# Moving VectorE's side steps next to the array steps in a two-layer mixture-of-experts and attention kernel

## The chip, the cores and the metric

The kernel runs on one core of a Trainium2 chip, in float32. The metric is the device time of one execution in microseconds (us), given as the median of several runs. The names used below: PE is TensorE, DVE is VectorE, ACT is ScalarE, POOL is GpSimd, and SP is the engine that issues most of the DMAs.

## The reference

The program is one "macaron" block on an input of 8 batches of 1024 tokens with 256 features each: half a feed-forward layer, attention, and half a feed-forward layer again, each on a layer-normed input and added to the residual.

```python
x = x + 0.5 * ffn(layernorm(x), ...)
x = x + attn(layernorm(x), ...)
x = x + 0.5 * ffn(layernorm(x), ...)

# attn: 16 heads of 16 features
xd = (x @ W_down).reshape(b, t, h, s)
keys, queries, values = per-head 16x16 products of xd      # keys and queries times 16 ** -0.25
attn = softmax(einsum('bqhs,bkhs->bhqk', queries, keys))
out = einsum('bhqk,bkhs->bqhs', attn, values) @ W_unify + b_unify

# ffn: each token goes to its best of 8 experts, which takes its first 320 tokens in order;
# the rest of the tokens go through a shared two-layer network
eid = argmax(softmax(xf @ router_w + router_b))
rank = place of the token among those of its expert
out = expert(xf) where rank < 320 else shared(xf)
```

## The kernel before, in words

**Three parts in a row.** The first feed-forward layer, the attention of all batches, and the second feed-forward layer. The change lies in the attention part, in `run` inside `attention`. It runs over 32 *pairs* `n`: pair `n` is batch `n // 4` and one of its 4 groups of four heads. Each pair has 16 *units* `u`, two halves of 8, and in each unit the program issues:

- for pair `n`, twelve matmuls `psc` (the scores of four heads for 128 keys and 512 queries, three matmuls each), followed on ACT by four exponentials `ex` of 128x512;
- for the next pair `n + 1`, eight matmuls `pm` of the same kind (the scores the other way round, so that the maximum over the keys can be taken along a row), followed on DVE by four reductions `halves`, one for each `pm` tile of 128x512;
- for the unit before, the four products `av` with the values (`weighed`), either in one piece of 512 columns, or in two of 256.

A unit is written out in two half units: `ORDERS[0]` (heads 0 and 1 of `psc`, 2 and 3 of `pm`), then `av`, then `ORDERS[1]` (the other heads), then the second piece of `av` or an array step. Tiles `psc` rotate through four PSUM banks, and tiles `pm` through three. The three banks of `pm` are shared with some array steps: the router's logits `pl`, the routing sums `places` and `behind`, and the output projection `pu` each take one.

At the start of each half of a pair (units 0 and 8) DVE also transposes and inverts the finished `av` (`turned`, `rec`, in `divide`), and for the second and fourth group of a batch transposes the scaled result once more (`ho`, one unit later). At the end of each half it forms the minima (`lowest`, three small instructions, then `lowturned`).

**Work beside the pairs.** Everything else in this part is a set of generators in a list `beside`: `prepare(b)` (projections of the next batch), `unify(b)` (output projection), `route(b)` (layer norm, router and slots of the second feed-forward layer for a finished batch), `stats(b)` (layer norm statistics of a later batch) and `biased(b)`. Each generator yields the kind of its next step: ARRAY (it begins with PE), DVE or POOL. `step(kind)` advances the most urgent generator that stands at this kind, and does nothing when there is none. `queue(n)` adds them: `unify` and `prepare` in a batch's first pair, `route` of the batch before in its second pair, to be done four pairs later. `done_by(n)` at the end of a pair runs whatever is overdue. After the last pair `done_by(PAIRS + G)` runs what is left of the last `route`, and then the second half of the last batch's `unify` is issued and the second feed-forward layer begins.

A `route(b)` is a fixed string of steps: eleven DVE steps of layer norm (`norm_steps`: eight with `bn_stats` and `bn_aggr`, three with four or six small instructions each for the inverse root), two POOL steps (four rows are normalized, L184), six ARRAY steps (transposes `ptrn`, `pl`, `pl` with `logits`, for each of two halves), two DVE steps (`top`, `hot`; then `best`, `chosen`), an ARRAY step (`places`, with `sums` on POOL and `place` on DVE), two DVE steps (`rank`, `past`, `counted`; then `row`), an ARRAY step (`behind`, with `sums` on POOL again), a DVE step (`slot`, `lost`), and eight POOL steps that send the rows out by indirect DMA.

**What sets the order.** PE, ACT and DVE run their instructions in the order in which the program issues them here (a manual schedule); only POOL and SP are ordered by the framework. A DVE step therefore stands behind the reductions of its unit and in front of those of the next.

**Which unit runs which step.** Before, `SLOTS_OF` holds two sets for each pair: units (modulo 8) for an ARRAY step and units for a DVE step. For the first two pairs of a batch these are 0, 1, 3, 5 and 2, 4, 6; for the last two pairs 0, 1, 4 and 2, 3, 5, 6. A unit without an ARRAY step runs a POOL step. In the last pair of all (`ahead` is false, there is no `pm` any more) each unit from 2 on runs an ARRAY step.

Of the kernel before, what the change touches and what calls it, by code (L numbers as in the profile page):

```python
# [21 lines left out]
TB = T // P  # L22
# [18 lines left out]
def macaron(  # L41
# [98 lines left out]
    ARRAY, DVE, POOL = 0, 1, 2  # L140
# [620 lines left out]
    def attention(use, weights, router):  # L761
# [11 lines left out]
        PAIRS, UNITS = B * G, 2 * TB  # L773


        SLOTS_OF = [((0, 1, 4), (2, 3, 5, 6)), ((0, 1, 3, 5), (2, 4, 6))]

        ORDERS = [
            [(kind, int(h)) for kind, h in order.split()] for order in (
# [139 lines left out]
        def fetch(n):  # L919

            b, g = divmod(n, G)
            rows = slice(g * 64, (g + 1) * 64)
            qt = qts[n] = use.pool.tile([P, T], F32R, tag=f"q{n % 3}", name=f"q_{n}")
            kt = kts[n] = use.pool.tile([P, 2, T], F32R, tag=f"k{n % 3}", name=f"k_{n}")
            for i in range(2):
                nc.sync.dma_start(
                    out=kt[:, i, :].bitcast(F32), in_=krows[b][i, rows].rearrange("r c t -> (r c) t")
                )
            nc.sync.dma_start(out=qt.bitcast(F32), in_=qrows[b][rows].rearrange("r c t -> (r c) t"))
# [79 lines left out]
        def weigh(n, u, exs, parts=(0, 1)):  # L1009

            b, g = divmod(n, G)
            q, c = divmod(u, TB)
            if (n, q) not in avs:
                avs[n, q] = use.av.tile([P, 512], F32, tag="av", name=f"av_{n}_{q}")
            cols = slice(256 * parts[0], 256 * (parts[-1] + 1))
            for h, ex in enumerate(exs):
                at = (c * HEADS + 4 * g + h) * V
                nc.tensor.matmul(  # L1018
                    avs[n, q][32 * h : 32 * h + 32, cols],
                    lhsT=vps[b % 2][:, at : at + 2 * S],  # L1020
                    rhs=ex[:, cols],
                    start=(c == 0),
                    stop=(c == TB - 1 and parts[-1] == 1),
                )
            if c == TB - 1:
                divide(n, q)
# [30 lines left out]
        def unify(b, start=0):  # L1057
            for t in range(start, TB, 2):
                ps = bank_v(f"pu_{b}_{t}")
                for i in range(2):  # L1060
                    q, at = divmod((t + i) * P, 512)
                    for g in range(G // 2):
                        nc.tensor.matmul(  # L1063
                            ps[:, i * D : (i + 1) * D],
                            lhsT=outs[b, g, q][:, at : at + P],
                            rhs=wu_sb[:, g, :],
                            start=(g == 0),
                            stop=(g == G // 2 - 1),
                        )
                two = xs[b][:, t : t + 2, :]  # L1070
                nc.vector.tensor_tensor(
                    two, two, ps.rearrange("p (t d) -> p t d", d=D), ALU.add
                )
                rows = slice(b * T + t * P, b * T + (t + 2) * P)
                nc.sync.dma_start(
                    out=ahead_of_last[rows].rearrange("(t p) d -> p t d", p=P), in_=two
                )
                yield
# [48 lines left out]
        def afterwards(n=0):  # L1127

            for _ in range(len(later) - n):
                later.pop(0)()  # L1130
# [5 lines left out]
        def due(kind):  # L1136
            return min((w for w in beside if w[1] == kind), key=lambda w: w[0], default=None)

        def step(kind):
            work = due(kind)  # L1140
            if work is None:
                return
            try:
                work[1] = next(work[2]) or ARRAY
            except StopIteration:
                beside.remove(work)

        def done_by(n):
            while any(by <= n for by, _, _ in beside):
                for kind in (POOL, DVE, ARRAY):  # L1150
                    if any(by <= n and what == kind for by, what, _ in beside):
                        step(kind)

        def queue(n):

            b, g = divmod(n, G)
            if n + 2 < PAIRS:
                fetch(n + 2)
            if 0 < n <= B - AHEAD + 1:

                again = AHEAD - 2 + n
                nc.vector.memset(xs[again][:, 0, :1], 0.0)
                reload(again)
                beside.append([G * (again - 1) - 1, DVE, stats(again)])
            if g == 0:
                if b > 0:
                    beside.append([n, ARRAY, unify(b - 1)])
                if b + 1 < B:
                    beside.append([n + 1, POOL, prepare(b + 1)])
            if g == 1 and b > 0:  # L1170
                beside.append([n + 4, DVE, route(b - 1)])

        def ones(i):
            vp = use.pool.tile([P, TB * HEADS * V + S], F32, tag=f"vp{i}", name=f"vp{i}")
            nc.gpsimd.memset(vp, 1.0)
            vps.append(vp)

        def zero_rows(i):
            m = use.pool.tile([P, 512], F32R, tag=f"m{i}", name=f"m{i}")
            nc.gpsimd.memset(m.bitcast(F32), 0.0)  # L1180
            ms.append(m)
# [48 lines left out]
        def run(own):  # L1230
            for i in range(2, 4):
                zero_rows(i)
            fetch(1)
            ones(1)
            last = None

            def weighed(parts=(0, 1)):
                if last is not None:
                    weigh(*last, parts=parts)

            for n in range(PAIRS):
                ahead = n + 1 < PAIRS
                if n == (B - 1) * G:
                    done_by(n)
                    use.pool = own
                    use.last.close()
                    router.open()

                queue(n)
                for u in range(UNITS):  # L1250
                    todo = {}
                    old = len(later)
                    slots = SLOTS_OF[n % G < 2]
                    if ahead:
                        passes(n, n + 1, u, ORDERS[0], todo)

                        other = u % TB in slots[0] and due(ARRAY) is not None

                        whole = other or u % TB < 2
                        weighed((0, 1) if whole else (0,))  # L1260
                        passes(n, n + 1, u, ORDERS[1], todo)
                        if other:
                            step(ARRAY)
                        elif not whole:
                            weighed((1,))
                    else:

                        passes(n, None, u, ORDER_OF_LAST, todo)
                        weighed()
                        other = False  # L1270
                        if u > 1:
                            step(ARRAY)
                        if u == TB + 3:
                            beside.append([n + 1, ARRAY, islice(unify(B - 1), 2)])
                    if u % TB in slots[1]:
                        step(DVE)
                    if not other:
                        step(POOL)
                    last = (n, u, [todo["ex", h] for h in range(4)])
                    afterwards(len(later) - old)  # L1280
                    if ahead and u % TB == TB - 1:
                        lowest(n + 1, u // TB)
                if ahead:
                    done_by(n)
            weighed()
            afterwards()
            done_by(PAIRS + G)
            for _ in unify(B - 1, TB // 2):
                pass
# [17 lines left out]
    use = Use()  # L1307
    weights, fill_weights = attention_weights(const)
    first_pair, run = attention(use, weights, layers[1])

    def beside_last(blocks, main):
# [102 lines left out]
```

## Time and profile before

| | |
|---|---|
| median of 3 runs | 2935.99 us (2933.0 to 2938.25) |
| the profiled execution | 2939.6 us, its span 2937.9 us |
| first `ex` of pair 0 | 662.2 us from the span's start |
| first `ex` of pair 31 | 2399.7 us |
| last `ex` | ends at about 2449.4 us |
| busy share of PE, DVE, ACT, POOL | 95%, 64%, 47%, 29% |
| mean granted TensorE clock | 0.981 |

The times of the profile are those of one execution, which was 3.6 us longer than the median. The attention part takes some 1790 us of the span. In it each pair takes between 49 and 61.5 us, and the length of a unit can be read from the starts of the `ex` instructions on ACT: two in a row after each half unit. A pair with `prepare` or `unify` steps takes 58 to 61 us, one with some steps of `route` 52 to 55 us, and one with DVE steps alone about 50 or 51 us. Busy shares of PE are those of matmuls whose ends are modelled, so a unit's length says more than they do.

### The profile page before, as it was taken

How to read it: one execution, taken by the hardware profiler on the slowest of the kernel's cores; microseconds unless marked ns; L12 is line 12 of the kernel's file. 1: busy time of each engine (PE TensorE's matmuls, PEld its weight loads, DVE VectorE, ACT ScalarE, POOL GpSimd, SP SyncE). 2: the span in 40 equal slices, each digit the busy share in tenths (PEclk: the TensorE clock that was granted, in tenths of full speed). 3: DMA queues.
4: the chain of work that ended last, by engine and by line, in shares of the span. 5: the costliest groups of instructions: out<-in, count | busy, mean ns of one | idle time of the engine just before them, and what ended most of it. 6: DMA issues, size and time to landing. Idle time of an engine off the chain costs nothing.

```text
span 2937.9 us, 56693 instructions
## 1 busy us (share of the span) xinstructions
PE 2799.3 (95%) x22066; PEld 1546.2 (53%) x22066; DVE 1883.1 (64%) x4189; ACT 1375.2 (47%) x2512; POOL 851.8 (29%) x1136
## 2 busy tenths in 40 slices
PE   4799999899999999999999999999999999999998
PEld 4567776454444444444444444444444445666775
DVE  7344223467897888888788788788788963212221
ACT  1111111207766666766766765766766663111111
POOL 3434433414001033123222321420420214432331
PEclk7799999999999999999999999999999999999999
DMA  7522553413112101301301301311321102321440
GB/s 224 152 83 78 176 187 99 161 47 121 53 58 97 67 24 60 124 24 56 128 24 52 133 24 42 125 41 39 125 80 38 39 3 73 128 61 49 150 147 28
DMA packets 163737, 251.47 MB, mean 86 GB/s; under 512 B 36737, under 2 KB 109698, under 8 KB 163458
## 3 DMA queue, kind: packets, MB, share of 16 engines
q1 hardware_dynamic: 144178, 196.93, 20.6%
q0 software_dynamic: 18432, 50.62, 5.1%
q8 instruction: 177, 2.90, 0.4%
q14 instruction: 102, 0.84, 0.1%
q10 hardware_dynamic: 848, 0.18, 0.0%
HBM read 144.10 MB, written 103.57 MB: 84 GB/s over the span
## 4 chain that ended last, share of the span: by engine, by line
PE 63%; DVE 13%; issue 1%; DMA 0%; POOL 0%; ACT 0%; POOLq 0%; DVEq 0%
PE psc L987 20%; PE av L1018 15%; DVE halves L1003 9%; PE pm L987 6%; PE pe_o L499 5%; PE ph_o L456 5%; PE pe_e L499 2%; PE ph_e L456 2%; PE pu L1063 2%; PE pxd L862 2%; PE pv L894 1%; DVE turned L1033 1%; PE pq L880 1%; PE pl L1091 1%; PE ptrn L832 0%
## 5 line engine op out<-in xcount | busy, mean ns | idle before, releaser
L1003 DVE TENSOR_REDUCE halves<-pm 128x1 f32<-128x512 f32 x2048 | 1309.3, 681 | 260.9 <-PE pm L987 239.6
L996 ACT ACTIVATE ex<-psc 128x512 f32<-128x512 f32 x2048 | 1111.4, 596 | 574.5 <-PE psc L987 570.9
L987 PE MATMUL pm<-k,q 32*128 32x512 f32 x4096 | 870.5, 448 | 50.6 <-DVE halves L1003 38.6
L987 PE MATMUL psc<-q,k 32*128 32x512 f32 x4096 | 791.8, 455 | 3.1 <-PEq L668 3.1
L1018 PE MATMUL av<-ex,vp 128*32 128x256 f32 (+1 forms) x6472 | 610.9, 449 | 0.0
L987 PEld LDWEIGHTS psc<-q,k 32*128 32x128 f32 x4096 | 326.6, 183 | 479.0 <-issue 423.1
L987 PEld LDWEIGHTS pm<-k,q 32*128 32x128 f32 x4096 | 374.9, 183 | 133.4 <-DVE halves L1003 107.3
L987 PE MATMUL psc<-m,ones_r 32*128 32x512 f32 x2048 | 406.9, 390 | 0.0
L456 PE MATMUL ph_o<-bT_o,oa 128*128 128x512 f32 x704 | 318.6, 601 | 7.1 <-DVE h_o L474 5.3
L499 PE MATMUL pe_o<-ob,h_o 128*128 128x256 f32 x1408 | 322.6, 386 | 0.0
L1041 POOL TENSOR_TENSOR ot<-turned,rec 128x256 f32<-128x256 f32 x64 | 39.7, 620 | 883.9 <-DVE rec L1036 875.6
L499 PEld LDWEIGHTS pe_o<-ob,h_o 128*128 128x128 f32 x1408 | 268.1, 193 | 48.5 <-issue 13.8
L1018 PEld LDWEIGHTS av<-ex,vp 128*32 128x32 f32 x6472 | 127.6, 108 | 298.3 <-issue 275.6
L456 PEld LDWEIGHTS ph_o<-bT_o,oa 128*128 128x128 f32 x704 | 131.2, 191 | 159.7 <-issue 147.4
L470 ACT ACTIVATE h_o<-ph_o,ob 128x512 f32<-128x512 f32 x88 | 60.5, 687 | 328.9 <-PE ph_o L456 305.0
L987 PEld LDWEIGHTS psc<-m,ones_r 32*128 32x128 f32 x2048 | 196.6, 184 | 13.0
L474 DVE TENSOR_SCALAR h_o<-ph_o,ob 128x512 f32<-128x512 f32 x88 | 65.9, 748 | 196.2 <-ACT h_o L470 179.4
L509 DVE SCALAR_TENSOR_TENSOR y_o<-pe_o,old_o 128x256 f32<-128x256 f32 x88 | 37.2, 423 | 205.8 <-PE pe_o L499 141.2
L499 PE MATMUL pe_e<-wb,h_e 128*128 128x256 f32 (+1 forms) x640 | 143.9, 381 | 0.0
L456 PE MATMUL ph_e<-bT_e,wa 128*128 128x320 f32 x512 | 140.6, 433 | 1.8 <-ACT bT_e L204 1.8
L204 ACT COPY bT_o<-pt_bT_o 128x1024 f32<-128x1024 f32 x22 | 22.3, 1012 | 250.8 <-PE pt_bT_o L200 225.9
L499 PEld LDWEIGHTS pe_e<-wb,h_e 128*128 128x128 f32 (+1 forms) x640 | 112.9, 179 | 16.4 <-issue 3.1
(183 smaller groups left out, 2385.1 us busy)
## 6 DMA issues: line engine op xcount, KB each, us to landing
k<-krows SPq DMA_DIRECT2D x64, 512.0 KB
wa<-in_w_dram SPq DMA_DIRECT2D x16, 1024.0 KB
wb<-in_w_dram SPq DMA_DIRECT2D x16, 1024.0 KB
krows<-kh SPq DMA_DIRECT2D x32, 512.0 KB
krows<-kl SPq DMA_DIRECT2D x32, 512.0 KB
q<-qrows SPq DMA_DIRECT2D x32, 512.0 KB
rows_o<-buf SPq DMA_DIRECT2D x88, 130.0 KB
x<-in_x_dram SPq DMA_DIRECT2D x8, 1024.0 KB
```

Source lines behind the costliest of these rows:

```text
L456: nc.tensor.matmul(ps[:, i * 512 : i * 512 + width], lhsT=wa[:, k, (m + i) * P : (m + i + 1) * P], rhs=xnt[:, k, c0:c1], start=(k == 0), s ...
L470: nc.scalar.activation(t[:, 0, : hi - lo], ps[:, lo - c0 : hi - c0], AF.Relu, bias=bias[:, m : m + 1],)
L474: nc.vector.tensor_scalar(t[:, 1, : hi - lo], ps[:, 512 + lo - c0 : 512 + hi - c0], bias[:, m + 1 : m + 2], 0.0, ALU.add, ALU.max,)
L499: nc.tensor.matmul(ps[lo - i * P : hi - i * P, :D], lhsT=of[:, lo - a : hi - a], rhs=w[:, m, :], start=(m == 0), stop=(m == MC - 1),)
L509: nc.vector.scalar_tensor_tensor(y[:n, :], ps[:n, :D], 0.5, olds[i][:n, :], ALU.mult, ALU.add)
L862: nc.tensor.matmul(ps, lhsT=wd_sb[:, k, m * P : (m + 1) * P], rhs=xnt[:, k, :], start=(k == 0), stop=(k == KC - 1),)
L987: nc.tensor.matmul(ps, lhsT=lhs, rhs=rhs, start=(len(left) + 1 == todo[kind, h, "of"]), stop=not left,)
L996: nc.scalar.activation(ex, ps, AF.Exp, scale=S ** -0.5)
L1003: nc.vector.tensor_reduce(halves[m][:, t, half, h : h + 1], ps, AX.X, ALU.max, negate=True)
L1018: nc.tensor.matmul(avs[n, q][32 * h : 32 * h + 32, cols], lhsT=vps[b % 2][:, at : at + 2 * S], rhs=ex[:, cols], start=(c == 0), stop=(c == ...
L1041: nc.gpsimd.tensor_tensor(outs_t[q][:, :, at : at + S].rearrange("p (t a) s -> p a t s", t=4), by[:, :, :S].rearrange("p (a t) s -> p a t ...
L1063: nc.tensor.matmul(ps[:, i * D : (i + 1) * D], lhsT=outs[b, g, q][:, at : at + P], rhs=wu_sb[:, g, :], start=(g == 0), stop=(g == G // 2 - 1),
```

## The change

The two sets become one: units for an ARRAY step. A unit that runs an ARRAY step then also runs two DVE steps, right after it. Any other unit runs a DVE step only at position 6 of a half (modulo 8), and in the last pair of all at each odd unit as well. In a batch's last two pairs the ARRAY units are 0 and 1 of each half, no longer 4. When no ARRAY step is due in a unit, `other` is false, and the unit runs no DVE step except at position 6.

```diff
-        SLOTS_OF = [((0, 1, 4), (2, 3, 5, 6)), ((0, 1, 3, 5), (2, 4, 6))]
+        SLOTS_OF = [(0, 1), (0, 1, 3, 5)]
...
-                        other = u % TB in slots[0] and due(ARRAY) is not None
+                        other = u % TB in slots and due(ARRAY) is not None
...
-                    if u % TB in slots[1]:
+
+                    if other:
+                        step(DVE)
+                        step(DVE)
+                    elif u % TB == TB - 2 or not ahead and u % 2:
                         step(DVE)
                     if not other:
                         step(POOL)
```

`TB` is 8, and `slots` is `SLOTS_OF[n % G < 2]` with `G` = 4. No instruction is added or taken away; the steps of the generators run in other units.

## The prediction

> **What bounds the kernel now.** The page first: busy shares, the chain that ended last, the costliest groups.
>
> ```profile
> PE 2799.3 (95%) x22066; PEld 1546.2 (53%) x22066; DVE 1883.1 (64%) x4189; ACT 1375.2 (47%) x2512; POOL 851.8 (29%) x1136
> ...
> PE 63%; DVE 13%; issue 1%; DMA 0%; POOL 0%; ACT 0%; POOLq 0%; DVEq 0%
> ...
> L1003 DVE TENSOR_REDUCE halves<-pm 128x1 f32<-128x512 f32 x2048 | 1309.3, 681 | 260.9 <-PE pm L987 239.6
> ...
> L987 PE MATMUL pm<-k,q 32*128 32x512 f32 x4096 | 870.5, 448 | 50.6 <-DVE halves L1003 38.6
> ```
>
> PE leads, and DVE is the only other engine on the chain, through `halves`. Next the timeline of ACT in pair 23, whose `ex` starts mark the half units:
>
> ```profile
> 1997.08 1.09 ACT L996 ACTIVATE ex<-psc 128x512 f32<-128x512 f32 x2 [0.35 <-PE psc L987]
> 1998.53 1.09 ACT L996 ACTIVATE ex<-psc 128x512 f32<-128x512 f32 x2 [0.37 <-PE psc L987]
> 2000.01 1.08 ACT L996 ACTIVATE ex<-psc 128x512 f32<-128x512 f32 x2 [0.40 <-PE psc L987]
> ...
> 2005.29 1.08 ACT L996 ACTIVATE ex<-psc 128x512 f32<-128x512 f32 x2 [0.84 <-PE psc L987]
> ...
> 2008.90 1.08 ACT L996 ACTIVATE ex<-psc 128x512 f32<-128x512 f32 x2 [0.35 <-PE psc L987]
> ```
>
> A quiet half unit is 1.47 us, a unit 2.94. Two reductions take 1.29, so DVE has 0.36 us per unit to spare, less than one `bn_stats` step (0.42 + 0.18). Unit 13, from 2005.29 to 2008.90, is 3.61 long. The timeline of DVE and PE says why:
>
> ```profile
> 2003.09 1.29 DVE L1003 TENSOR_REDUCE halves<-pm 128x1 f32<-128x512 f32 x2 [0.48 <-PE pm L987]
> 2004.30 0.20 DVE L236 COPY sums<-places 128x56 f32<-128x56 f32 x1
> 2005.73 0.22 DVE L308 TENSOR_TENSOR place<-sums,places 128x64 f32<-128x64 f32 x1 [1.23 <-POOL sums L238]
> 2005.87 2.58 DVE L1003 TENSOR_REDUCE halves<-pm 128x1 f32<-128x512 f32 x4
> 2006.61 0.18 PEld L987 LDWEIGHTS pm<-k,q 32*128 32x128 f32 x1 [0.36 <-DVE halves L1003]
> ```
>
> A `places` step holds DVE for 1.23 us while it waits for POOL. The next reductions stand behind it, the first ends at about 2006.5, and the second `pm` of the half unit after gets its bank only then. That is the mechanism to follow: DVE work between two sets of reductions costs PE nothing until it delays a reduction by more than about 0.3 us; beyond that it costs its length.
>
> **The change part by part.** I take each step's units from the order of the two programs. No instruction or DMA is added. For one batch (routing of batch b-1):
>
> (a) *Layer norm steps, pair 4b+1.* Before in units 2, 4, 6, 10, 12, 14 and on into the next pair; now two each in units 0, 1, 3, 5, 8 (beside `prepare`), one in 6. A `prepare` unit is 4.7 to 4.85 long, since the array step adds about 1.9 us of PE. Of this DVE has 1.5 idle: two steps of 0.60 fit. Unit 5 is only 3.94: I count 0.5 for it and the two after it. In unit 8, with `turned` and `rec` (0.71 + 0.25), the two long steps (six instructions of 0.17, 1.0 us each) spill 0.4. Before, these units cost nothing (2.80 to 3.08). Sum +0.9. No row shows two steps in such a unit: from 0 (all hidden) to 3 (five units by 0.6); I stay near 1 because the idle time can be read in the trace; less than nothing is excluded, as nothing is lost there now.
>
> (b) *Pair 4b+2 loses its DVE steps* (units 2, 3, 5, 6, 10) and gets four array steps in units 0, 1, 8, 9 instead of one in 12. By the `ex` starts, units of pair 22 with DVE work or its backlog took 3.22, 3.03, 3.59 and 3.57. New length, from units elsewhere with these steps: transposes 3.95 and 0.14 in the unit after, `pl` 3.80, `pl` in unit 8 4.21; 3.95 + (3.80 + 0.14) + 4.21 + 3.95 + 0.14 + 12 x 2.94 = 51.5, against 51.8: -0.3.
>
> (c) *Pair 4b* loses the `behind` step from unit 9 (3.79, now 3.19) and its DVE step from 10 (3.26, now 2.94): -0.9. POOL now sends rows before it normalizes for `prepare`: 4 x 1.22 us start at unit 7, wanted at 11; hidden, else the excess over 12 us.
>
> (d) *Pair 4b+3*: the routing chain in lumps. Unit 1: `logits`, `top`, `hot`, a wait for POOL's `hot` (0.32 and two hand-overs of about 0.1), `best`, `chosen`: 1.35 more between two sets of reductions; beyond the tolerance 1.1. Unit 8, behind `turned` and `rec`: `sums`, wait and `place` 1.65 (2004.30 to 2005.95), POOL's `place` 0.5, `rank` to `counted` 0.58, `row` 0.21; reductions start 2.5 late, PE stops 1.8. Unit 9: `behind` and its POOL wait 1.3 (2052.20 to 2053.50), `slot` and `lost` with a POOL wait 0.7, then `ho` 0.63: PE stops 1.6 once more. The next PE work in order is the second half's `psc`, so ACT idles too. Array steps are shorter than `pl` by some 0.6 in unit 9, none in 8. 8 and 9 together, by the start of unit 11's first matmuls, 3.5; all 4.6. Bounds: 0 (all absorbed), and 6 (1.35 + 2.5 + 2.1, no tolerance at all); the 0.67 us lost behind the 1.65 us step above stand nearest to my value. Length 4.24 + 3.80 + 4.21 + 3.80 + 12 x 2.94 + 4.6 = 55.9, against 54.0: +1.9.
>
> One late batch: +0.9 - 0.3 - 0.9 + 1.9 = +1.6; batches 3 to 6: +6.4. Batch 2 also loses `stats` steps from pairs 8, 10, 11 (59.4 to 58.4, 53.3 to 51.4, 54.7 to 55.9; pair 9 +0.9): -0.8. Batch 1: pair 4 puts two `stats` steps beside each `unify`, whose `pu` add on DVE (0.69) waits for the end of the array step, so that 1.2 us follow it: 0.6 to 1.0 by five units, less 1 for units relieved, +3.5; the others +0.9, +0.5, +0.8: +5.7. Batch 0: pairs 2 and 3 have no array work, so one DVE step per half instead of four: 51.1 and 51.0 to 49.5 each, pair 1 -0.5: -3.6. Batch 7: pairs 28 to 30 -0.9, -0.4, -2.9 (52.4 to 49.5), and six of seven array steps leave pair 31: -1.3: together -5.5. Loop: 6.4 - 0.8 + 5.7 - 3.6 - 5.5 = +2.2.
>
> (e) *The end.* In pairs 29 and 30 no array step is due, so the last routing moves by one DVE step per half. After the loop there remain seven array steps, five DVE steps and the sends; before, one DVE step and the sends.
>
> ```profile
> 2448.77 1.68 PE L1018 MATMUL av<-ex,vp 128*32 128x512 f32 x8
> ...
> 2452.99 3.29 PE L1063 MATMUL pu<-wu,ho 128*128 128x256 f32 x14 [1.04 <-DVE behind L339]
> ...
> 2453.49 0.74 DVE L184 TENSOR_SCALAR send<-x,mean,rstd 128x256 f32<-128x256 f32 x2
> ...
> 2463.90 3.70 PE L456 MATMUL ph_o<-bT_o,oa 128*128 128x512 f32 x8 [0.75 <-DVE h_o L474]
> ```
>
> PE finishes `av` at 2450.4 and goes on with `pu` at 2453.0. Now, in order, it must first do `pl` (2.1, hidden behind POOL's four rows of 1.22, which start at about 2449.1 and end at 2454.0), `ptrn` to 2454.8, two ACT copies of 0.6 to 2455.5, `pl` to 2457.6, `logits` to `hot` 2458.4, POOL 2458.9, `best`, `chosen` 2459.4, `places` 2460.0, `sums` and `place` 2461.7, POOL 2462.1, `rank`, `past` 2462.5, `behind` 2463.1. Then `pu`, which ran 1 us earlier in part: PE 10.8 late. DVE's sends start near 2465.5, 12.0 late; behind them stands `h_o`, which `ph_o` already waits for. POOL's gathers of old rows stand behind the sends and have the 19 us of `ph_o` and `pe_o` as cover. SP loads the next block's rows after the last send (2471.84), and PE wants them at 2488.31: both move together. So +12; from 9 (PE's lateness, less a shorter pair 31) to 14.
>
> Sum: 2.2 + 12 = +14.2.
>
> [...] The clock, in windows around the one long unit of pair 15:
>
> ```profile
> 1509.00:1513.00 4.00, 4.00 (x28) 1.39 (x21) 1.99 (x4) 1.32 (x3) 0.00 (x0) 0.57 0.08 17
> 1513.00:1530.00 17.00, 17.00 (x195) 8.78 (x197) 13.52 (x22) 12.45 (x24) 6.69 (x7) 1.00 0.01 2
> ```
>
> The granted clock fell to 0.57 over 4 us, and unit 1 of pair 15 took 5.30 where pairs 11 and 23 took 3.8. It followed a `pm` that had waited about 0.4 us; pair 19 has the same after such a stop. [...] I take one, +1.5.
>
> Total +15.7, say +16. On the profiled execution's own time, 2939.6, that is 2955.6; it stands 3.6 above the median, so 2952.
>
> **The rivals.** *The chain's waits are absorbed*, by banks and by the length of the array units (faster). Without the 4.6 us in batches 1 to 6 the total is 15.7 - 27.6 = -12: 2924. For it: most units with DVE steps, 2.90 to 3.08, show nothing lost. Against: unit 13 above lost 0.67 to a single wait. The total is zero where a batch's chain costs 2.0 us instead of 4.6. *The end is hidden*: if POOL's rows and the sends overlap what PE has left, (e) is 2 instead of 12, and the total +5.7: just under 2942, no change. Against: PE takes its matmuls in order. *Two steps are too many beside every array step*: (a) at 3 and pair 4 at 6 add 15 + 3, clock dips 3: 2973. *The change hardly acts*, because no array step is due: true of pairs 2, 3, 29 and 30 alone; elsewhere 14 of 16 steps of a batch move into twos.
>
> **How the numbers follow.** My forecast has 0.68 (own range 2943 to 2963), the slower rival 0.10, no gain at the end 0.12, the faster one 0.10. This kernel's measurement tells about 0.2%, 5.9 us, from no change: so 0.78 slower, 0.12 same, 0.10 faster. The range, 2936 to 2971, leaves out the faster rival and the far half of the slower one.
>
> **What would show it.** Right: unit lengths by `ex` of about 4.9 and over in units 2, 9 and 10 of pairs 7, 11, ..., 27; `LDWEIGHTS pm` there waiting 1 us and more for `halves`; pairs 2, 3 and 30 at 49.5; the first `pu` after the last `av` about 10 us later than before. Wrong: pair 23 at 54 or less, or `pu` within 5 us of the last `av`.

## The result: 2.6% slower, and the profile after

The changed kernel takes 3014.54 us (median, 3007.41 to 3015.26), the kernel before in the same series 2937.12: ratio 1.026, interval 1.024 to 1.0279. Predicted were 2952 us and slower. The sign was right, the size was not: +77 instead of +16.

The profiled execution after took 3007.4 us, its span 3005.7: 67.8 us above the profiled one of before. It was the fastest of its four runs, and that of before the slowest of its four, so the traces show 67.8 of the 77 us. The same lines of its page as were shown of before (the chain's shares by engine, then the groups of `halves` and `pm`):

```profile
PE 2857.2 (95%) x22218; PEld 1573.8 (52%) x22218; DVE 1896.0 (63%) x4189; ACT 1375.3 (46%) x2512; POOL 851.2 (28%) x1136
...
PE 60%; DVE 15%; POOL 1%; issue 1%; DMA 1%; ACT 0%; another core or an unknown queue 0%; POOLq 0%; DVEq 0%; ACTq 0%
...
L1003 DVE TENSOR_REDUCE halves<-pm 128x1 f32<-128x512 f32 x2048 | 1312.3, 683 | 296.2 <-PE pm L987 282.8
...
L987 PE MATMUL pm<-k,q 32*128 32x512 f32 x4096 | 889.9, 455 | 62.3 <-DVE halves L1003 44.6
```

DVE does the same 4189 instructions in nearly the same time (1896 us against 1883), yet its share of the chain rose from 13 to 15%, and it now waits 43 us more for `pm` (282.8 against 239.6). PE's matmuls of `pm` wait only 6 us more for `halves` (44.6 against 38.6), but PE's busy time rose by 58 us for the same matmuls (the trace of before has 152 records fewer; at PE's mean of 0.13 us for each they are some 20 of the 58): slow matmuls (sixteen of `pu` at half clock, 5.94 for 3.99) and those that start and then wait (two `pm` that took 0.50 us in before, at 2002.32, where no reduction held them, took 1.09 in unit 4 of pair 26, at full clock) count as busy. So two things are to be looked for, a wait that both engines share, and the clock.

Lengths by the `ex` starts, as sums over the four pairs of a batch, against the steps of the prediction:

| | predicted | measured |
|---|---|---|
| batch 0 | -3.6 | +6.3 (pair 1 +9.0) |
| batch 1 | +5.7 | +20.1 (pair 4 +7.0, pair 6 +8.4) |
| batch 2 | -0.8 | +5.6 |
| batches 3 to 6 | +6.4 | +28.3 |
| batch 7 | -5.5 | -5.5 |
| after the last `ex` | +12 | +15.1 |

The start of the first `ex` moved by -2.3, so the table adds up to the 67.8, but for rounding. Four places hold the loss.

**A bank of `pm` is held.** Timeline of ACT in pair 26 of after, units 4 to 7 (start, length, engine, operation, idle time before it and its releaser):

```profile
2199.81 1.09 ACT L996 ACTIVATE ex<-psc 128x512 f32<-128x512 f32 x2 [0.81 <-PE psc L987]
2201.71 1.08 ACT L996 ACTIVATE ex<-psc 128x512 f32<-128x512 f32 x2 [0.81 <-PE psc L987]
2203.61 1.08 ACT L996 ACTIVATE ex<-psc 128x512 f32<-128x512 f32 x2 [0.82 <-PE psc L987]
2205.51 1.09 ACT L996 ACTIVATE ex<-psc 128x512 f32<-128x512 f32 x2 [0.81 <-PE psc L987]
```

No array or DVE step runs here, but a half unit takes 1.90 us, not 1.47. Timelines of DVE and of the weight loads in the same units:

```profile
2199.51 1.29 DVE L1003 TENSOR_REDUCE halves<-pm 128x1 f32<-128x512 f32 x2 [0.61 <-PE pm L987]
2201.41 1.29 DVE L1003 TENSOR_REDUCE halves<-pm 128x1 f32<-128x512 f32 x2 [0.61 <-PE pm L987]
```

```profile
2200.85 0.18 PEld L987 LDWEIGHTS pm<-k,q 32*128 32x128 f32 x1 [0.42 <-DVE halves L1003]
...
2202.75 0.18 PEld L987 LDWEIGHTS pm<-k,q 32*128 32x128 f32 x1 [0.42 <-DVE halves L1003]
```

PE waits for `halves`, DVE waits for `pm`, in turn: 1.29 + 0.61 = 1.90. That is what the loop looks like with two banks instead of three. The third holds `pl`: its first half is written in unit 1, its second only in the next ARRAY unit, which was the neighbour before (units 0 and 1, or 8 and 9), and is unit 8 now. Units 2 to 7 of pair 26 take 22.80 us instead of the 17.64 of six quiet units (before, with DVE steps in them, they took 18.86). It is the same in pairs 6, 10, 14, 18 and 22: 5.2 us a batch against quiet units, some 31 in all.

**The chain, and the clock behind it.** Timeline of DVE around units 8 and 9 of pair 27:

```profile
2269.14 1.22 DVE L1003 TENSOR_REDUCE halves<-pm 128x1 f32<-128x512 f32 x2
2270.28 0.21 DVE L236 COPY sums<-places 128x56 f32<-128x56 f32 x1
2271.71 0.22 DVE L308 TENSOR_TENSOR place<-sums,places 128x64 f32<-128x64 f32 x1 [1.23 <-POOL sums L238]
2272.36 0.22 DVE L312 TENSOR_REDUCE rank<-place 128x8 f32<-128x64 f32 x1 [0.43 <-POOL place L310]
...
2273.12 2.55 DVE L1003 TENSOR_REDUCE halves<-pm 128x1 f32<-128x512 f32 x4
2275.59 0.16 DVE L236 COPY sums<-behind 128x7 f32<-128x7 f32 x1
2276.72 0.17 DVE L333 TENSOR_TENSOR behind<-sums,behind 128x8 f32<-128x8 f32 x1 [0.97 <-POOL sums L238]
...
2278.18 1.25 DVE L1003 TENSOR_REDUCE halves<-pm 128x1 f32<-128x512 f32 x2
```

These are the two lumps of the prediction, each with its waits for POOL inside it: no reduction runs from 2270.4 to 2273.1, and none from 2275.7 to 2278.2. Then the windows of the same stretch (length; busy PE, PEld, DVE, ACT, POOL; granted clock; DMA):

```profile
2265.00:2269.00 4.00, 4.00 (x48) 1.59 (x40) 3.72 (x10) 2.42 (x6) 0.00 (x0) 1.00 0.00 0
2269.00:2273.00 4.00, 3.41 (x24) 1.22 (x23) 2.31 (x10) 2.14 (x4) 2.17 (x6) 1.00 0.00 0
2273.00:2276.00 3.00, 2.08 (x17) 1.35 (x20) 2.73 (x7) 1.09 (x2) 0.47 (x3) 1.00 0.04 5
2276.00:2286.30 10.30, 9.81 (x73) 3.36 (x69) 6.23 (x13) 4.17 (x8) 7.94 (x13) 0.50 0.13 42
```

PE idles for 1.5 of the 7 us, and then runs at half clock for 10.2. Units 9, 10 and 11 take 5.51, 6.01 and 4.53. The same follows the chain in pairs 7, 11, 15, 19 and 23, for 6.8 to 13.7 us each. In the whole loop the clock is at half for 87 us, against 11 before.

**Pairs 1 and 4.** Timeline of DVE in unit 0 of pair 1:

```profile
720.73 1.22 DVE L1003 TENSOR_REDUCE halves<-pm 128x1 f32<-128x512 f32 x2
726.21 0.43 DVE L148 BATCH_NORM_STATS2 st_a<-x 128x6 f32<-128x256 f32 x1 [4.26 <-DMA x<-after_first]
```

The first `stats` step of a batch now stands in the first unit of the pair at whose start its rows are requested; DVE waits 4.26 us for the DMA, and the reductions behind it too. Half clock follows for 6.8 us, and once more in this pair for 3.4. In pair 4 (units 1 and 4 to 6 at 5.2, 5.3, 5.4 and 4.3) two `stats` steps stand beside each `unify`, and units 4 and 5 have 3.4 us of half clock.

**The end.** Timeline of PE after the last `av` (by which the loop ends):

```profile
2501.98 1.08 PE L1018 MATMUL av<-ex,vp 128*32 128x512 f32 x8
2503.00 1.95 PE L1091 MATMUL pl<-rw,Trn 128*128 128x8 f32 x16
...
2507.84 3.64 PE L1091 MATMUL pl<-rw,Trn 128*128 128x8 f32 x16 [0.29 <-ACT Trn L835]
...
2513.63 0.40 PE L306 MATMUL places<-chosen,ones_r 128*128 128x64 f32 x1
2516.64 0.38 PE L326 MATMUL behind<-past,before_r 128*128 128x8 f32 x1 [2.61 <-DVE past L314]
...
2517.30 5.94 PE L1063 MATMUL pu<-wu,ho 128*128 128x256 f32 x16
```

`pu` starts 14.2 us after the last `av` ends (before: in the main 2.5), as the prediction had it, and the second `pl` and `pu` run at half clock (3.64 for 1.95; 5.94 for 3.99).

### The profile page after: what moved, and what is told of

Its sections match the earlier page's. It is cut to its first block, busy times and chain, and to the rows that moved or that the text cites. A ratio compares the mean times of both kernels' runs of the same rounds, so it can differ in the third digit from the quotient of the medians.

```text
span 3005.7 us, 56997 instructions
## 1 busy us (share of the span) xinstructions
PE 2857.2 (95%) x22218; PEld 1573.8 (52%) x22218; DVE 1896.0 (63%) x4189; ACT 1375.3 (46%) x2512; POOL 851.2 (28%) x1136
## 4 chain that ended last, share of the span: by engine, by line
PE 60%; DVE 15%; POOL 1%; issue 1%; DMA 1%; ACT 0%; another core or an unknown queue 0%; POOLq 0%; DVEq 0%; ACTq 0%
PE psc L987 19%; PE av L1018 14%; DVE halves L1003 10%; PE pm L987 6%; PE pe_o L499 5%; PE ph_o L456 5%; PE pe_e L499 2%; PE ph_e L456 2%; PE pu L1063 2%; PE pxd L862 1%; PE pv L894 1%; PE pq L880 1%; DVE turned L1033 1%; DVE ho L1053 0%; PE ptan L832 0%
## 5 line engine op out<-in xcount | busy, mean ns | idle before, releaser
L1003 DVE TENSOR_REDUCE halves<-pm 128x1 f32<-128x512 f32 x2048 | 1312.3, 683 | 296.2 <-PE pm L987 282.8
L987 PE MATMUL pm<-k,q 32*128 32x512 f32 x4096 | 889.9, 455 | 62.3 <-DVE halves L1003 44.6
L987 PE MATMUL psc<-q,k 32*128 32x512 f32 x4096 | 818.2, 462 | 2.4 <-PEq L668 2.4
L1018 PE MATMUL av<-ex,vp 128*32 128x256 f32 (+1 forms) x6624 | 625.9, 450 | 0.0
L987 PE MATMUL psc<-m,ones_r 32*128 32x512 f32 x2048 | 413.0, 396 | 0.0
```

What stands on the lines that cost most here:

```text
L987: nc.tensor.matmul(ps, lhsT=lhs, rhs=rhs, start=(len(left) + 1 == todo[kind, h, "of"]), stop=not left,)
L1003: nc.vector.tensor_reduce(halves[m][:, t, half, h : h + 1], ps, AX.X, ALU.max, negate=True)
L1018: nc.tensor.matmul(avs[n, q][32 * h : 32 * h + 32, cols], lhsT=vps[b % 2][:, at : at + 2 * S], rhs=ex[:, cols], start=(c == 0), stop=(c == ...
```

## The experiments

All but two start from the changed kernel. Each ratio is to the kernel before, run beside it.

**1. pl in one piece** (x1)

```diff
-                    if i == 1:
-                        yield
```

> The changed kernel, with the two halves of a router product pl issued in one array step instead of two (the yield between them is taken out), so that its PSUM bank is never held from one array unit to the next. Theory held bank: in the changed kernel the first half of pl runs in unit 1 and its second half only in unit 8, so for six units only two of the three banks are left for pm, and each of units 2 to 7 of pairs 6, 10, 14, 18, 22, 26 takes 3.80 us instead of 2.94. Then these units fall back to about 2.94 here, pairs 10 to 26 of this kind from 56.5 to about 52, and the span from 3006 to about 2975. Rival, GpSimd's bias adds, which stand in units 2 to 6 of the same pairs, slow VectorE: they stay there, so units 2 to 6 stay at 3.80 and the span within 5 us of 3006.

Measured: 3015.71 us, 1.0247 (1.0225 to 1.0268). Units 4 to 7 of pair 26 fell to 2.93 to 2.94: the bank was what they waited for. Units 2 and 3 took 5.19 and 3.45, as half clock fell on them. The steps of `biased`, which are issued in the same units, are still there, so they are not the cause. The total did not move: half clock in the loop rose from 87 to 154.5 us, and the pair as a whole took 60.7 (56.5 in the changed kernel). The view of windows in pair 26 of this kernel:

```profile
2184.00:2190.00 6.00, 6.00 (x57) 2.83 (x55) 4.96 (x11) 4.22 (x8) 3.62 (x4) 1.00 0.65 251
2190.00:2197.00 7.00, 7.00 (x58) 4.01 (x60) 4.39 (x8) 3.26 (x6) 1.82 (x2) 0.67 0.02 4
```

and its timeline of PE at that place:

```profile
2189.94 1.95 PE L1091 MATMUL pl<-rw,Trn 128*128 128x8 f32 x16
```

Sixteen `pl` matmuls of 8 columns in a row, and the clock falls although PE counts as busy all the time.

**2. pl in a bank of psc** (x11)

```diff
-                pl = bank_v(f"pl_{b}_{q}")
+                pl = bank(f"pl_{b}_{q}")
```

> After, with the router's tile pl taken from the four banks of psc instead of the three of pm. Theory (the half-written pl holds one of three pm banks in units 2 to 7): these units of pairs 6, 10, ..., 26 fall from 3.80 to between 2.94 and 3.2 us, since psc needs two banks per half unit and has a third left; pair 26 at 52 to 53, about 4 us each, and as the matmuls of pl stay apart, no new dips of the clock: sum near 2990. Rival one (the time comes back as half clock, as when pl ran in one piece): pairs shorter in units 2 to 7 and longer elsewhere, sum above 3008. Rival two (psc suffers from three banks as pm from two): units 2 to 7 at 3.5 and more.

Measured: 2981.03 us, 1.0154 (1.0132 to 1.0176): some 31 us of the loss gone by the two ratios, each known to about 6 us. In the traces 24 us of it lie in the six pairs 6, 10, ..., 26. Pairs 10, 14, ..., 26 take 52.4 to 52.6 (56.4 to 57.2), and pair 26 has no half clock. Timeline of ACT in its units 2 and 3:

```profile
2177.75 1.09 ACT L996 ACTIVATE ex<-psc 128x512 f32<-128x512 f32 x2 [0.48 <-PE psc L987]
2179.36 1.08 ACT L996 ACTIVATE ex<-psc 128x512 f32<-128x512 f32 x2 [0.52 <-PE psc L987]
2180.92 1.09 ACT L996 ACTIVATE ex<-psc 128x512 f32<-128x512 f32 x2 [0.48 <-PE psc L987]
```

A unit is 3.17 long: `psc` with three banks loses 0.23 a unit where `pm` with two lost 0.86. The held bank is shown, and its price: units 2 to 7 of pair 26 take 19.06 in all, 3.7 less than in the changed kernel.

**3. Only the twos, with before's array slots** (x5)

```diff
-        SLOTS_OF = [(0, 1), (0, 1, 3, 5)]
+        SLOTS_OF = [(0, 1, 4), (0, 1, 3, 5)]
```

> The array sets of before ((0, 1, 4) in a batch's last pairs), the twos of after. First theory (a bank held by a half-written pl): pl's halves now stand in units 1 and 4, and in 9 and 12, so units 2, 3 and 10, 11 of pairs 6, 10, ..., 26 take 3.8 us and units 5 to 7 fall to 2.94; pair 26 stays near 56.5. The chain's lump moves to unit 12 of that pair and units 0 to 2 of the next, where PE stops; pairs 7, 11, ..., 27 are 1 to 3 us shorter, the pairs before them longer. Sum within 10 us of after: 3005 to 3020. Rival (the missing array slot is what costs, not the twos): pair 26 at 52, pair 27 at 54 to 55, sum near 2970.

Measured: 3005.16 us, 1.0213 (1.0188 to 1.0238). Units 2 and 3 of pair 26 take 3.81 and 3.80, units 5 to 7 2.90 to 2.95, units 10 and 11 3.79 and 3.81. The slow units stand exactly between the halves of `pl` and moved with them. Pair 26 is at 56.9, and pair 27, with the chain in its first units and two spells of half clock, at 63.4; pairs 7, 11, ..., 23 became 0.5 to 5.2 shorter, and pairs 6 and 10 3.1 and 6.3 longer. So the slot 4 that the change took out is not what costs: with it back, 2.1 of the 2.6% are still lost. What matters is how early the twos let the routing start: before, its array steps happened to fall so that both halves of `pl` were neighbours.

**4. Twos in the first pairs only** (x7)

```diff
-                    if other:
+                    if n % G > 1:
+                        if u % TB in (2, 3, 5, 6):
+                            step(DVE)
+                    elif other:
                         step(DVE)
                         step(DVE)
```

> The array slots of after; two DVE steps beside an array step only in a batch's first two pairs, and before's single DVE steps (units 2, 3, 5, 6 of a half) in its last two. Theory (the chain in lumps stops PE for more than a microsecond, and the clock halves after it): pairs 7, 11, ..., 27 go from about 58 to 54 or 55, no stretch of half clock in them, while pair 26 stays at 56.5 (the bank is still held). The last routing again moves by four steps a half, so the tail is about 491 us. Sum near 2980. Rival (the clock is lost to the array steps' small matmuls alone, not to the chain): pair 27 stays above 57, and the sum above 2995.

Measured: 2984.01 us, 1.0156 (1.0127 to 1.0184). Pairs 7, 11, 15, 19 and 23 take 51.4 to 51.5 without half clock, pair 27 52.9 with one spell of 3.4 us. That is below the 54 expected because `behind` now runs in the next pair, which is 1.7 longer in pairs 12, 16 and 20, and 3.2 in pairs 8 and 24 with one spell of 3.4 us in each. Units 2 to 7 of pair 26 stay at 3.80, and the tail falls from 504.3 to 494.0. In pairs 7 to 23 the chain's lumps and the clock after them went together: spread out, neither is left. In pair 28 it is not so: there PE stops for 0.73 and 0.80 us around the `behind` step, 13.7 us at half clock follow, and the pair takes 62.8 (55.3 in the changed kernel). Timeline of ACT in pair 27 from its start, and the windows of its unit 0, the spell, and what follows:

```profile
2216.30 1.08 ACT L996 ACTIVATE ex<-psc 128x512 f32<-128x512 f32 x2 [0.38 <-PE psc L987]
...
2220.53 1.08 ACT L996 ACTIVATE ex<-psc 128x512 f32<-128x512 f32 x2 [1.25 <-PE psc L987]
2223.93 1.08 ACT L996 ACTIVATE ex<-psc 128x512 f32<-128x512 f32 x2 [2.31 <-PE psc L987]
2225.82 1.09 ACT L996 ACTIVATE ex<-psc 128x512 f32<-128x512 f32 x2 [0.81 <-PE psc L987]
```

```profile
2216.30:2220.40 4.10, 4.00 (x40) 2.06 (x36) 3.58 (x9) 2.17 (x4) 0.62 (x1) 1.00 0.89 349
2220.40:2223.80 3.40, 3.40 (x22) 0.99 (x19) 1.45 (x3) 1.08 (x2) 0.00 (x0) 0.50 0.08 13
```

This one spell gives a price of the clock. Unit 1, from 2220.53 to 2225.82, runs at half clock for 3.4 us, and takes 5.29 instead of the 3.80 of unit 1 in the other five pairs: 0.44 us lost for each us at half clock.

**5. Extra matmuls where PE stops** (x8)

```diff
+        def fill(n, u):
+            ps = bank(f"fill_{n}_{u}")
...
+            for _ in range(6):
+                nc.tensor.matmul(
...
+                        if n % G == 3 and n > 4 and u in (TB + 1, TB + 2):
+                            fill(n, u)
                         passes(n, n + 1, u, ORDERS[1], todo)
```

Each `fill` is six matmuls of 32x512 into one of the four banks of `psc`.

> After, with six extra matmuls of 32x512 (1.3 us of work whose result nothing reads) ahead of the second half unit of units 9 and 10 in pairs 7, 11, ..., 27, where PE stops for about 1.25 us. Theory (the stop itself brings the half clock): no half clock in these pairs, unit 10 at 4.9 instead of 6.0 and unit 11 at 3.0 to 3.3 instead of 4.5; 2.5 to 3.5 us less in each of six pairs, sum near 2996 although work was added. Rival (half clock comes from a cause outside PE's stop, or the long units are DVE's alone): units 9 to 11 as after or longer by the added work, sum 3014 to 3030.

Measured: 3016.93 us, 1.0263 (1.0236 to 1.029): nothing gained. Windows in pair 19, and then in pair 27:

```profile
1804.40:1813.20 8.80, 8.53 (x65) 4.14 (x63) 6.98 (x19) 4.34 (x8) 2.55 (x8) 1.00 0.01 2
1813.20:1830.30 17.10, 17.10 (x111) 7.39 (x111) 8.81 (x17) 6.25 (x12) 12.60 (x19) 0.50 0.12 41
...
2277.90:2292.00 14.10, 13.78 (x114) 6.78 (x110) 10.84 (x29) 6.50 (x12) 6.02 (x16) 1.00 0.06 18
```

With the stop filled (8.53 of 8.80 us busy) the clock still fell in five of six pairs. Where it did not, in pair 27, the pair took 55.2, against 58.8 to 62.0 in the other five with the same instructions and 10.2 to 17.1 us at half clock. That is what the clock is worth, 0.35 to 0.40 us for each us at half clock, but not what starts it: my narrow theory, that the one long stop does, failed here. Short stops ahead of the other `pm` and the small matmuls of `places` and `behind` were left in place.

**6. Routing sums on DVE** (x2)

```diff
-            yield from router.places(b, logits, use.pool, bank_v, nc.gpsimd)
+            yield from router.places(b, logits, use.pool, bank_v, nc.vector)
```

> The changed kernel, with the small sums of the routing chain (sums, place, start, row, behind, seen, lost) of the attention part on VectorE instead of GpSimd, so that VectorE no longer waits for GpSimd inside a step. Theory wait for GpSimd: VectorE's waits of 1.2 and 1.0 us before place and behind and the shorter ones before rank, row and slot go, while some 2 us of VectorE work come in; units 9 to 11 of pairs 7, 11, ..., 27, which now take 5.5, 6.0 and 4.5 us, fall to about 4.5, 4.5 and 3.5, some 3 us per batch, and the end of the loop gains 2 us: about 2985 from 3006. Rival, the lump itself (so many VectorE instructions in a row, whoever does the sums): no change or longer, 3006 to 3012.

Measured: 3007.65 us, 1.0212 (1.0186 to 1.0238). Pairs 7, 11, ..., 27 are mixed, 54.9 to 62.6, with up to 20.5 us of half clock in one. Without the waits for POOL the lumps are still there, as DVE then does the additions itself.

**7. The end as before** (x3): from pair 29 on, the sets of before for array and DVE steps (`SLOTS_WERE`).

```diff
+                        slots = SLOTS_WERE[n % G < 2][0] if n > 28 else slots
...
-                    if other:
+                    if n > 28:
+                        if u % TB in SLOTS_WERE[n % G < 2][1]:
+                            step(DVE)
+                    elif other:
```

> The changed kernel, but pairs 29 to 31 use the sets of units of the kernel before, so the last batch's routing is done within the last pairs again. Theory flush at the end: the stretch from the last exponential to the end, 15 us longer in the changed kernel, goes back to that of before, while pairs 29 to 31 are 4 us longer: 2995 from 3006. Rival, the 15 us come from a lower clock or from the transfers at the start of the last part: span within 4 us of 3006.

Measured: 3004.29 us, 1.0203 (1.0172 to 1.0234). The tail is 489.6 (before 489.2, after 504.3), pairs 29 to 31 are 4.1 longer: -11 net in the traces.

**8. No stats step before the rows are there** (x4)

```diff
                     if other:
-                        step(DVE)
-                        step(DVE)
+                        if n != 1 or u > 1:
+                            step(DVE)
+                            step(DVE)
```

> The changed kernel, but in pair 1 no VectorE steps stand beside the array steps of units 0 and 1, so the first statistics of batch 4 come after its load has landed. Theory wait for the load: VectorE waits 4.3 us for the DMA of x in unit 0 of pair 1, and the unit there takes 11.1 us where it took 4.7; here it is back to 4.7 and pair 1 from 64.9 to about 58, the span about 6 us lower, 3000. Rival, two statistics steps beside an array step are too much by themselves: units 3 and 5 of pair 1, which have them too, get as long, and the span stays within 2 us of 3006.

Measured: 3004.78 us, 1.0204 (1.0181 to 1.0226). The first statistics of pair 1, by the timeline of DVE, now start without a wait:

```profile
738.83 0.42 DVE L148 BATCH_NORM_STATS2 st_a<-x 128x6 f32<-128x256 f32 x1
```

Pair 1 went from 64.9 to 56.2.

**9. All four causes taken away at once** (x13): `pl` in a bank of `psc` for batches 0 to 5, single DVE steps in a batch's last two pairs, up to pair 4 none beside the array steps of units 0 and 1 of a half and one beside the others (in pair 0 none at all), the end as before. So this takes back much of the change; what stays is the array sets up to pair 28 and the twos in the first two pairs of a batch from pair 5 on.

```diff
-                pl = bank_v(f"pl_{b}_{q}")
+                pl = (bank if b < B - 2 else bank_v)(f"pl_{b}_{q}")
...
+                    elif n % G > 1 and n > G:
+                        if u % TB in (2, 3, 5, 6):
+                            step(DVE)
                     elif other:
-                        step(DVE)
-                        step(DVE)
+                        if n > G:
+                            step(DVE)
+                            step(DVE)
+                        elif u % TB > 1 and n:
+                            step(DVE)
```

> After with all four causes taken away at once, and the rest of the change kept (array slots 0 and 1 in a batch's last pairs, twos in pairs 5, 8, 9, ...): pl in a bank of psc for batches 0 to 5; single DVE steps in the last pairs; no DVE step in units 0 and 1 of pair 1 and one instead of two beside the other array steps of pairs 1 and 4; and the sets of before from pair 29 on. Theory (the four add up to nearly all of the loss: about 33 for the bank, 20 for the chain, 10 for pair 1, 10 for the end, a few for pair 4): 2926 to 2945, no measurable difference to before or a little faster; pair 26 at 52.5, pair 27 at 51.5, pair 4 near 61, tail near 490, little half clock in the loop. Rival (they overlap, or another cause of 15 us and more is left): 2955 and above.

Measured: 2936.44 us against 2941.33, 0.9986 (0.9973 to 0.9998). From the page of this kernel (its lines are numbered one higher):

```profile
PE 65%; DVE 11%; issue 1%; POOL 1%; DMA 1%; ACT 0%; POOLq 0%; DVEq 0%
...
L1004 DVE TENSOR_REDUCE halves<-pm 128x1 f32<-128x512 f32 x2048 | 1311.5, 682 | 246.0 <-PE pm L988 218.9
```

DVE's share of the chain is 11%, under the 13% of before, and half clock in the loop is at 11.8 us. So the loss lies in the parts that were taken away: nothing is left of it that these runs can tell from before (a gain like that of experiment 10 could hide a few us). Pair 4 is at 61.6 (66.9 after); its statistics moved on into pair 8, beside `unify` there, two at a time, and pair 8 went to 67.8 (58.3 after): the price of two `stats` steps beside `unify`, with one spell of 6.8 us at half clock in it.

**10. One part of the change on the kernel before** (x9)

```diff
+                        if n % G == 2 and G < n < PAIRS - G and u != TB + 4:
+                            other = False
...
-                    if u % TB in slots[1]:
+                    if n % G == 1 and G < n < PAIRS - G:
+                        if other:
+                            step(DVE)
+                            step(DVE)
+                        elif u % TB == TB - 2:
+                            step(DVE)
+                    elif u % TB in slots[1]:
                         step(DVE)
```

> Before, with one part of the change alone: in the second pair of batches 1 to 6 (pairs 5, 9, ..., 25) two DVE steps beside each array step; and in the pair after it no array step but the one in unit 12, so that the router's halves stay in neighbouring units as before. Theory: the layer norm steps beside the projections cost 0.2 to 0.6 us in pairs 5, 9, ..., 25 and leave pairs 6, 10, ..., 26 without VectorE steps, which saves 1 to 1.7 us each; no bank is held, no chain in lumps: 4 to 8 us faster than before, 0.997 to 0.999. Rival (twos beside array steps themselves stop PE and lower the clock): pairs 5, 9, ..., 25 gain 1 us or more each, sum 5 us above before.

Measured: 2932.81 us (2928.16 to 2938.62) against 2940.96, 0.9975 (0.9962 to 0.9987). It beats both kernels, the one before by 0.25%. Pairs 10, 14, ..., 26 take 50.2 to 50.3 (51.8 to 53.3 before), pair 25 61.4 (60.9). The gain lies in units 7 and 11 of pair 26, which took 3.56 each with a long norm step and are now 2.94.

**11. The same with the routing sums on DVE** (x10)

```diff
-            yield from router.places(b, logits, use.pool, bank_v, nc.gpsimd)
+            yield from router.places(b, logits, use.pool, bank_v, nc.vector)
```

> The kernel with norm steps in twos, and the routing sums (sums, place and the running sums of behind) formed on DVE instead of POOL, so that DVE does not wait 1.23 us for POOL in units 12 and 13. Theory: the stop of 0.67 us and the dips of the clock after it in pairs 15 and 19 go; pairs 7, 11, ..., 27 are 0.7 to 1.5 us shorter, the sum 8 to 16 us below before, ratio 0.995 to 0.998. Rival (the additions cost DVE as much as the wait did): pairs unchanged, no difference to the kernel with norm steps in twos.

Measured: 2931.31 us, 0.9972 (0.9961 to 0.9983): no difference to the one above. Unit 13 of pair 27 fell from 3.61 to 3.20, and unit 14 rose from 2.99 to 3.60. The rival was right: where DVE waited 1.23 us for POOL, it now spends 0.74 on the three additions itself, and later parts of the chain became DVE's too.

## Why the prediction was right or wrong

- *The mechanism to follow* (DVE work delays a reduction, and PE loses its length) held wherever DVE work is what changed, but it was followed too narrowly: the reductions also need banks, and a bank can be taken by an instruction of PE that no engine is busy with.
- *(a) Norm steps in twos*, +0.9 a batch: pairs 13, 17, 21 and 25 moved by -0.1 to +0.5 (pair 5 by +1.3). Right, a little high. The rival that two steps are too many beside every array step is wrong for these; it holds beside `unify`, in pair 4 (predicted +3.5, measured +7.0; pair 8 of experiment 9 shows it again).
- *(b) Pair 4b+2*, -0.3: measured +4.6 to +5.4 in pairs 14, 18, 22 and 26, +3.1 in pair 10 and +8.4 in pair 6. This is the step that failed. It priced the units with array steps from rows elsewhere and called the other twelve quiet, "12 x 2.94". Six of them lie between the halves of `pl` and took 3.80. A bank kept between two steps was put at nothing, without a reason. Everything needed was in the program: `pl` shares the three `pm` banks, and yields between its halves. Experiments 1 to 3 show the cause.
- *(c) Pair 4b*, -0.9: measured -0.9 to -1.0 in pairs 12, 16, 20 and 24. Right.
- *(d) The chain in lumps*: the stops came where they were put, in units 9 and 10; unit 1's cost 0.6 instead of 1.1 (unit 2 at 3.57, not the 4.9 given as a sign). So the waits are not absorbed, as the faster rival had it. The pairs took 57.1 to 58.3, predicted 55.9, but that they came so near is in part luck. With the chain spread out they take 51.4 (experiment 4), with it 57.9 in the mean, and the 9.7 us at half clock in each are some 3.7 of that at 0.38 us for each. So the stops themselves cost about 2.8 and not 4.6 (an estimate), and the clock makes up for it and more.
- *The clock*, +1.5: mis-sized most. At 0.35 to 0.44 us for each us at half clock (experiments 5 and 4), 76 us more of it in the loop are 27 to 33 us (an estimate; part of it lies in pairs 1 and 6). I had priced the chance of a dip by stops of 0.4 us (before, the clock fell after two of the 75 waits of PE for `halves`), and counted one to three for 18 new stops of over a microsecond. No run shows that count: all six chains had a spell, and it lasted not 3.4 us, which the 1.5 stood for, but 6.8 to 13.7. The rows gave a price of 1.5 us for one dip, from the one long unit of pair 15, and every chain was going to bring a longer one: the clock cost some thirty.
- *Batch 0*, pair 1 at -0.5: measured +9.0. Not seen: a step moved forward can overtake the DMA that feeds it. The SP queue of a moved step has to be looked at for what it needs too, not only for what it issues. Experiment 8 shows it. Half clock of 10.2 us in the pair is part of the 9.0.
- *Batch 7*, -5.5: measured -5.5. *(e) The end*, +12: +15.1; `pu` 11.7 us later where 10.8 was worked out, and `pl` and `pu` 3.6 longer at half clock. Both right in kind, and the rival of a hidden end is out; in the second the clock is missing again. Pairs 2, 3 and 30 at 49.4, 49.3 and 49.9 are as forecast.

Set pair by pair against the forecast of +15.7, the 67.8 us of the profiled execution part from it in five places: pairs 6, 10, ..., 26 with the held bank 33 us, pair 1 9.5, pairs 7, 11, ..., 27 with the chain 9, pair 4 3.5, the end 3. The rest comes out 6 us lower, of which 2.3 are the earlier start and 1.5 the allowance for the clock. The 27 to 33 us of the clock are no sixth place: they lie inside these, most of them in the pairs with the chain, where the stops cost less than forecast. With these parts of the change taken back together (experiment 9) the loss was gone. What stays open is what sets the clock: spreading the chain kept it up in five pairs of six, filling the longest stop did not in five pairs of six. The last section has what the traces show ahead of a fall.

## What to carry to other kernels

When work that yields in the middle is moved, ask for each stretch between its parts what it keeps hold of (a bank, a buffer), and price the units in between, not only the units in which it runs. A step that moves to an earlier place must be held against the DMA that feeds it. And where PE is the bound, price waits that are gathered in a few units with the clock after them: here they cost about 2.8 us a pair by themselves and some 3.7 at half clock (the estimates above), and spread out neither in five pairs of six, though in three of the six pairs after, into which the `behind` step moved on, there was half clock (3.4, 3.4 and 13.7 us).

## What the runs showed of the hardware that was not expected

Half clock came in spells of 3.4, 6.8, 10.2, 13.7 and 17.1 us, multiples of the shortest. And it came while PE counted as busy: in experiment 1 the clock was at 0.67 over 7 us in which PE counted as busy for 7.00, after a row of sixteen 8-column matmuls; in experiment 5 it fell to 0.50 after 8.8 us with 8.53 busy, most of it matmuls on 32 rows. So PE's idle time alone does not tell when the clock falls.

The traces of the changed kernel and of the kernel before show what stood ahead of a fall. In each of the two, the changes between full and half clock lie whole multiples of 3.413 us apart, to within 0.02 us. Take the stretches of the loop between these points, 0.2 us early, and count in each the matmuls that start in it, each as its columns times the share that its weights (32x128 in `psc` and `pm`, 128x32 in `av`) have of 128x128, the largest in the traces. In the changed kernel the clock fell after 11 stretches, with counts from 1408 to 2752 and a median of 2048; it stayed up after 502, with a median of 4032, and 21 of these have 2752 or less (without the 0.2 us the two part less well: 77 of the 502 are then at or under the highest count ahead of a fall). Before, it fell after two, with 2624 and 2368, and stayed up after 518, with a median of 3968, and 4 of these have 2624 or less. By PE's busy share the falls are parted less well: in the changed kernel 97 of the 502 are at or under the highest share ahead of a fall (0.97; the median ahead of a fall is 0.61), and before, both falls came with 0.97. So a low count went with a fall more closely than a low busy share. This was read from the traces afterwards, no run was made to test it, and what sets the clock was not shown.

The price was 0.35 to 0.44 us for each us at half clock (experiments 5 and 4).
